# A graph attention kernel: the edge features' products as two halves of 64 rows, in steps of four tiles

## The chip, the cores and the metric

The kernel runs on one core of a Trainium2 chip. A core has five engines, each with its own queue of instructions that it works off in order: TensorE (PE in the profile; its weight loads are listed apart as PEld), VectorE (DVE), ScalarE (ACT), GpSimd (POOL) and SyncE (SP), which here only issues DMAs. Semaphores hold an instruction back until another engine or a DMA has finished. Matmuls read SBUF and write PSUM, a memory of eight banks, each 2 KB on each of 128 partitions (512 f32 values). The metric is the time of one execution on the device in microseconds.

## The reference

One layer of a graph network. There are 12500 nodes with 128 features and 412500 edges, sorted by their target `dst`. Cut to what matters:

```python
h = relu(layernorm(x))
q, k, v = h @ Wq + bq, h @ Wk + bk, h @ Wv + bv        # per node
eh = edge_attr_64 @ We + be                            # per edge, 64 features
attn_in = concat([q[src], k[dst], eh], axis=-1)
hmid = leaky_relu(attn_in @ A1 + b1, 0.2)
scores = leaky_relu(hmid @ A2 + b2, 0.2)               # 8 heads
w = softmax(scores.mean(axis=-1), axis=0)              # over all edges
out = segment_sum(w[:, None] * v[dst], src)            # per source node
y = h @ Wn + bn + out
return x + gamma * (y - mean(y)) / sqrt(var(y) + 1e-5) + beta
```

The product with `A1` is linear, so the kernel folds it into the weights: `Wq`, `Wk` and `We` are multiplied by their part of `A1` once, and an edge's hidden row is the sum of a row for the source, a row for the target and the edge features times a 64x128 matrix.

## The kernel before

Edges are cut into tiles of 128, and eight tiles make a group (`SUPER`); there are 403 groups. Four chunks of 86, 121, 121 and 75 groups (`CHUNKS`) are worked on one after the other.

After a prologue (weights, indices, L243 to L338) and the per-node products (`nodes`, L529), the main part runs in five stages, c = 0 to 4 (the loop at L982). Each stage interleaves several jobs, written as Python generators:

- `first_stage(c)` (L631) makes, for each edge of chunk c, a row of 257 numbers: the place of the source within its block, 128 hidden values (target's part plus edge features' part) and 128 values `v[dst]`. The row is scattered into a table in HBM (`tab`), sorted by source.
- `second_stage` (L692) reads the table of chunk c-1 back block by block, adds the source's part, applies the leaky ReLUs, the heads and a running softmax, and sums the weighted values per source node.
- `ready` (L513) works out ahead, for chunk c+1 (in stage 0 also for what is left of chunk 0), in which slot of the table every edge goes: `count`, `plan`, `place_slots`. Its matmuls are at L459, DVE's reduction of them at L503 and the next selection at L452.
- `clear_ends` clears the ends of the next table.

`interleave` (L61) gives each job a number of steps and always runs the one that is proportionally furthest behind, up to its next `yield`. The order that comes out is the order of the instructions on PE, DVE, ACT and SP (`manual_schedule`, L996). `first_stage` has four yields for a group of eight tiles, in the kernel before and after the change.

A group's data are loaded two groups ahead (`load`, L640): `ea_t`, the edge features, transposed on the host, with tiles 0 to 3 of the group in partitions 0 to 63 and tiles 4 to 7 in partitions 64 to 127; `kv`, a window of target rows, each f32 number split into three bf16 parts; and `offs`, from which DVE makes the 0/1 matrix `sel` (L657).

One step of `first_stage` (L674 to L689) handles two tiles, k and k+4 of the group. The weight matrix `w_ea` has the shape [128, 2, 128] and is block diagonal: the folded 64x128 matrix stands in rows 0 to 63 for the first 128 columns and in rows 64 to 127 for the second, with zeros elsewhere (L241, L257). So one matmul of 128 rows with 256 columns (L679) gives the edge part of both tiles, in one PSUM bank (`row_ps`, two buffers, L610). Two bf16 matmuls with `sel` (L682) add the targets' part and the values. An f32 matmul is carried out as two weight loads and two passes, so L679 has two records for each matmul. `Later` (L80) holds the eviction back by one step: at the start of the next step `evict` (L660) issues on ACT a copy of the places (L662) and a copy of the whole bank (L665) into a row buffer (`pr`, seven buffers), and POOL issues two scatters (L621).

Of the other work, these lines matter here. Second stage, on PE: `turn` L738 and L741, the heads L758, `by_slot` L775, `turn_top` L792, `spread_top` L799, `products` L833. On ACT: `steep` L749, the exponentials L810. On DVE: L750.

## Time and profile before

| | |
|---|---|
| median of 11 runs | 6851.04 us (6835.54 to 6861.52) |
| profiled execution, its own time | 6852.19 us |
| its span in the profile | 6850.4 us |
| mean granted TensorE clock | 0.88 of full speed |
| stage 0: first stage of chunk 0, `ready` | 470 to 1510 us |
| stage 1: first stage of chunk 1, second of chunk 0, `ready` | 1515 to 3110 us |
| stage 2: first stage of chunk 2, second of chunk 1, `ready` | 3115 to 4780 us |
| stage 3: first stage of chunk 3, second of chunk 2 | 4785 to 5930 us |
| stage 4: second stage of chunk 3, then the ending | 5930 to 6850 us |

The stages' limits are read from the first and last L679 of each chunk. How to read the lines: a line of groups gives the source line, engine, operation, tiles (out<-in), form and number of instructions, then the busy time in us, the mean duration in ns, and the engine's idle time just before these instructions with what ended most of it. A line of the windows gives start and end, length, then the busy us and number of instructions of PE, PEld, DVE, ACT and POOL, the granted clock, the share of the DMA engines and GB/s. A line of the timeline gives start and duration in us, engine, line, operation and number; in brackets stands the idle time before it. A line of the waits gives who waited for whom: us in total, times, and the longest. The recorded duration of a matmul includes the tail of its pipeline, so matmuls that follow each other overlap in the records; what a matmul costs in a stream is the distance from start to start.

### The profile page before, as it was taken

What the parts mean: (1) busy time and instruction counts of PE and PEld (TensorE: products, weight loads), DVE (VectorE), ACT (ScalarE), POOL (GpSimd) and SP (SyncE); (2) the same over time, 40 slices, a digit from 0 to 9 for tenths busy, and PEclk for the clock granted to TensorE, in tenths of its full rate; (3) what the DMA queues carried; (4) which work ended last, traced back from release to release, by engine and by line L of the source; (5) the groups of instructions that cost most, each with busy time, mean ns of one, the idle gap of its engine ahead of it and who ended that gap; (6) DMA issues with size and microseconds to landing.
All of it is one profiled execution on the core that took longest, in us unless ns stands there. A gap on an engine that the chain in (4) does not pass through costs nothing. (4 is left out here: it accounts for less than half of the span.)

```text
span 6850.4 us, 98826 instructions
## 1 busy us (share of the span) xinstructions
PE 5186.3 (76%) x31430; PEld 3515.3 (51%) x31788; DVE 4548.1 (66%) x14001; ACT 2187.3 (32%) x5624; POOL 3370.3 (49%) x3236
## 2 busy tenths in 40 slices
PE   0555566558877878788888888777999999888881
PEld 0223343325555555556555555555666666656651
DVE  4875565546666666666666666665777777777778
ACT  0442222223333333333333333333333333333331
POOL 0017667765666666665566665655555555300000
PEclk9777767767889988898999998998999999999995
DMA  9344445556777777676777777776777887644443
GB/s 184 124 164 152 151 136 159 154 154 198 213 213 217 217 214 212 212 218 208 225 235 240 236 241 218 225 223 202 241 252 248 250 257 246 200 153 153 150 145 113
DMA packets 607898, 1362.10 MB, mean 199 GB/s; under 512 B 120437, under 2 KB 337197, under 8 KB 569353
## 3 DMA queue, kind: packets, MB, share of 16 engines
q1 hardware_dynamic: 423284, 877.57, 45.5%
q0 software_dynamic: 154704, 424.26, 17.3%
q10 hardware_dynamic: 29380, 53.87, 2.3%
q8 instruction: 252, 4.13, 0.3%
q14 instruction: 278, 2.27, 0.1%
HBM read 782.14 MB, written 573.14 MB: 198 GB/s over the span
## 5 line engine op out<-in xcount | busy, mean ns | idle before, releaser
L621 POOL DMA_INDIRECT tab<-row,slots x3223 | 3368.6, 1045 | 2545.0 <-issue 827.0
L665 ACT ACTIVATE row<-row_ps 128x512 f32<-128x512 f32 x1612 | 952.0, 591 | 1514.5 <-PE row_ps L682 625.5
L679 PE MATMUL row_ps<-w_ea,ea_t 128*128 128x256 f32 x3224 | 1117.0, 432 | 97.6 <-ACT row L665 55.2
L833 PE MATMUL o_ps<-rows_of,w 128*128 128x128 f32 x7252 | 1121.9, 298 | 76.4 <-DVE w L824 55.1
L750 DVE TENSOR_TENSOR rows_of<-h_ps,low 128x512 f32<-128x512 f32 (+1 forms) x980 | 635.4, 648 | 658.5 <-ACT low L749 406.5
L824 DVE TENSOR_SCALAR w<-iota_f,rows_of,score 128x128 f32<-128x128 f32 x3626 | 1021.6, 351 | 9.5
L833 PEld LDWEIGHTS o_ps<-rows_of,w 128*128 128x128 f32 x7252 | 945.5, 200 | 120.1 <-DVE w L824 76.7
L749 ACT ACTIVATE low<-h_ps 128x512 f32<-128x512 f32 (+1 forms) x980 | 551.1, 562 | 1118.0 <-PE h_ps L741 548.1
L679 PEld LDWEIGHTS row_ps<-w_ea,ea_t 128*128 128x128 f32 x3224 | 628.9, 215 | 465.2 <-issue 206.3
L741 PE MATMUL h_ps<-sel_q,qw 128*128 128x512 bf16 (+1 forms) x2582 | 738.7, 373 | 24.0 <-issue 3.4
L503 DVE TENSOR_REDUCE num<-run 128x5 f32<-128x500 f32 x646 | 433.8, 672 | 416.1 <-remote 227.2
L682 PE MATMUL row_ps<-kv,sel 126*128 126x256 bf16 x3224 | 682.7, 296 | 17.4 <-DMA ea_t<-in_ea 15.7
L758 PE MATMUL s_ps<-rows_of,a_sb 128*32 128x512 f32 (+1 forms) x1960 | 522.9, 625 | 139.2 <-DVE most_of L805 69.2
L738 PE MATMUL h_ps<-ident,rows_of 128*128 128x128 f32 x3626 | 591.5, 284 | 0.9 <-issue 0.9
L459 PE MATMUL run<-one,rest_b 128*128 128x500 f16 x642 | 278.3, 433 | 354.2 <-DVE num L503 246.5
L738 PEld LDWEIGHTS h_ps<-ident,rows_of 128*128 128x128 f32 x3626 | 451.8, 147 | 110.9 <-issue 86.4
L682 PEld LDWEIGHTS <-sel 126*128 126x128 bf16 x3224 | 346.3, 107 | 313.4 <-issue 93.4
L775 PEld LDWEIGHTS s_ps<-heads,z 96*128 96x128 f32 (+1 forms) x3136 | 392.4, 194 | 217.3 <-DVE z L769 151.8
L775 PE MATMUL s_ps<-heads,z 96*128 96x3 f32 (+1 forms) x3136 | 411.1, 252 | 109.4 <-DVE z L769 86.0
L765 ACT ACTIVATE z<-s_ps,b_col 64x512 f32<-64x512 f32 (+1 forms) x392 | 267.5, 682 | 639.5 <-PE s_ps L758 376.3
L452 DVE TENSOR_TENSOR one<-bins_b,block 128x500 f16<-128x500 bf16 x646 | 431.3, 668 | 1.7 <-PE run L459 1.6
L769 DVE SCALAR_TENSOR_TENSOR z<-z 64x512 f32<-64x512 f32 (+1 forms) x392 | 267.4, 682 | 223.1 <-ACT z L765 192.0
(172 smaller groups left out, 4860.2 us busy)
## 6 DMA issues: line engine op xcount, KB each, us to landing
rows_of<-tab SPq DMA_DIRECT2D x196, 1413.5 KB
ea_t<-in_ea SPq DMA_DIRECT2D x403, 256.0 KB
tab<-blank SPq DMA_DIRECT2D x392, 257.0 KB
rows_of<-tab SPq DMA_DIRECT2D x98, 1028.0 KB
rows_of<-tab SPq DMA_DIRECT2D x98, 899.5 KB
tab<-row,slots POOLq DMA_INDIRECT x3223
offs<-off_d SPq DMA_DIRECT2D x403, 126.0 KB
qw<-q_tab SPq DMA_DIRECT2D x392, 96.0 KB
```

The lines of the kernel that those rows point to most:

```text
L621: i = nc.gpsimd.indirect_dma_start(out=tabs[c][:, :], out_offset=bass.IndirectOffsetOnAxis(ap=slots[c][t // (8 * STR)][:m, t % (8 * STR):t ...
L665: nc.scalar.activation(row[:, :, 1:ROW], bank, AF.Copy)
L679: nc.tensor.matmul(bank[:, :, 0:D], lhsT=ea_g[:, ts(k, P)], rhs=w_ea, start=True, stop=False, skip_group_check=True)
L682: nc.tensor.matmul(bank[:, b, :], lhsT=sel[:, ts(b * halves + k, P)], rhs=kv, start=False, stop=True, skip_group_check=True)
L738: nc.tensor.matmul(h_ps[:, ts(j, P)], lhsT=rows_of[i][:, q * QUAD + j, 1:D + 1], rhs=ident, is_transpose=True, start=j == 0, stop=False, s ...
L741: nc.tensor.matmul(h_ps[:, 0:m * P], lhsT=qws[i][:, ts(k, D)], rhs=plss[i][:, q * QUAD * P:(q * QUAD + m) * P], start=False, stop=k == 2, ...
L749: nc.scalar.activation(low, h_ps, AF.Copy, scale=SLOPE)
L750: nc.vector.tensor_max(rows_of[i][:, q * QUAD:q * QUAD + m, 1:D + 1], h_ps.rearrange("p (j e) -> p j e", j=m), low.rearrange("p (j e) -> p ...
L758: nc.tensor.matmul(state["s_ps"][32 * q:32 * (q + 1), 0:m * P], lhsT=a2_sb, rhs=rows_of[i][:, q * QUAD:q * QUAD + m, 1:D + 1], start=True, ...
L775: nc.tensor.matmul(state["s_ps"][:, 0:nq * QUAD].rearrange("p (q j) -> p j q", j=QUAD)[:, j, :], lhsT=state["z"][:32 * nq, ts(j, P)], rhs= ...
L824: nc.vector.tensor_scalar(w, iota_f, rows_of[i][:, t, 0:1], state["score", i][:, t:t + 1], op0=ALU.is_equal, op1=ALU.mult)
L833: nc.tensor.matmul(state["o_ps"][:, 0:D], lhsT=w, rhs=rows_of[i][:, t, D + 1:ROW], start=t == 0, stop=t == ct - 1)
```

## The change

`w_ea` becomes [128, 128]: the folded 64x128 matrix stands in rows 0 to 63 and again in rows 64 to 127, without zeros. A step handles four tiles, k, k+1 and k+4, k+5, with k = 0 or 2. Each tile has its own f32 matmul of 64 rows and 128 columns: tiles k and k+1 use the lower 64 rows of the array and write the first bank, tiles k+4 and k+5 use the upper 64 rows and write the second. They are issued alternately, lower, upper, lower, upper; the four bf16 matmuls follow. A step has two yields: after the first one the two banks are evicted, each with two ACT copies and two scatters. The number of buffers, loads, bf16 matmuls, evictions and scatters is as before, `row_ps` still has two buffers, and the loads and the selection stay at the same yield of a group. In `other_edges` only the slice of `w_ea` is written differently.

```diff
-    w_ea = const.tile([P, 2, D], FP, name="w_ea")
+    w_ea = const.tile([P, D], FP, name="w_ea")
...
-    nc.vector.memset(w_ea, 0.0)
...
-        for b in range(2):
-            nc.vector.tensor_copy(w_ea[b * DE:(b + 1) * DE, b, :], fold[b * DE:(b + 1) * DE, 2, :])
+        nc.vector.tensor_copy(w_ea, fold[:, 2, :])
...
         def evict(g, k, bank):
             row = pr.tile([P, 2, ROW], FP, name="row")
-            nc.scalar.activation(row[:, :, 0:1],
-                                 place1[:, g * SUPER:(g + 1) * SUPER].rearrange("p (b k) -> p b k", b=2)[:, :, k:k + 1],
-                                 AF.Copy)
+            nc.scalar.activation(row[:, :, 0:1], place1[:, g * SUPER + k:g * SUPER + k + 2].unsqueeze(2), AF.Copy)
             nc.scalar.activation(row[:, :, 1:ROW], bank, AF.Copy)
-            for b in range(2):
-                scatter(c, g, b * halves + k, row[:, b, :], sent)
+            for j in range(2):
+                scatter(c, g, k + j, row[:, j, :], sent)
...
-            for k in range(halves):
-                later.step()
+            for k in range(0, halves, 2):
 
                 ea_g, kv, sel = got[g]
-                bank = ps_row.tile([P, 2, 2 * D], FP, name="row_ps")
-                nc.tensor.matmul(bank[:, :, 0:D], lhsT=ea_g[:, ts(k, P)], rhs=w_ea, start=True, stop=False,
-                                 skip_group_check=True)
+                banks = [ps_row.tile([P, 2, 2 * D], FP, name="row_ps") for _ in range(2)]
+                for j in range(2):
+                    for b in range(2):
+                        nc.tensor.matmul(banks[b][:, j, 0:D], lhsT=ea_g[b * DE:(b + 1) * DE, ts(k + j, P)],
+                                         rhs=w_ea[b * DE:(b + 1) * DE, :], start=j == 0, stop=False,
+                                         skip_group_check=True)
                 for b in range(2):
-                    nc.tensor.matmul(bank[:, b, :], lhsT=sel[:, ts(b * halves + k, P)], rhs=kv, start=False, stop=True,
-                                     skip_group_check=True)
-                later.after(1, lambda g=g, k=k, bank=bank: evict(g, k, bank))
+                    for j in range(2):
+                        nc.tensor.matmul(banks[b][:, j, :], lhsT=sel[:, ts(b * halves + k + j, P)], rhs=kv, start=False,
+                                         stop=True, skip_group_check=True)
                 if k == 0 and g + 2 < g0 + n:
                     load(g + 2)
-                if k == 1 and g + 1 < g0 + n:
+                yield
+                for b in range(2):
+                    evict(g, b * halves + k, banks[b])
+                if k == 0 and g + 1 < g0 + n:
                     select(g + 1)
                 yield
-        yield from later.rest()
```

More of the change, by code (lines that the diff above doesn't have):

```diff
@@ L77, in some_steps @@
         yield
-class Later:
-    def __init__(self):
-        self.now = 0
-        self.todo = {}
-    def after(self, steps, job):
-        self.todo.setdefault(self.now + steps, []).append(job)
-    def step(self):
-        self.now += 1
-        for job in self.todo.pop(self.now, []):
-            job()
-    def rest(self):
-        while self.todo:
-            self.step()
-            yield
 @with_exitstack
@@ L635, in first_stage @@
         win_v = kv_tab.rearrange("n (s d) -> (n s) d", s=3)
-        later = Later()
         got = {}
@@ L942, in other_edges @@
                     nc.tensor.matmul(bank[:, 0:D], lhsT=ea_t[b * DE:(b + 1) * DE, ts(j, P)],
-                                     rhs=w_ea[b * DE:(b + 1) * DE, b, :], start=True, stop=True)
+                                     rhs=w_ea[b * DE:(b + 1) * DE, :], start=True, stop=True)
                     nc.vector.tensor_add(hid, hid, bank[:, 0:D])
```

## The prediction

> **What bounds the kernel now.** I read the page first, then the busy time by stretch (one stretch for each of the five stages of the main part), the waits, and last the order of time around the products that change. The chain that ended last covers only the closing normalisation, so it does not help here.
>
> ```profile
> PE 5186.3 (76%) x31430; PEld 3515.3 (51%) x31788; DVE 4548.1 (66%) x14001; ACT 2187.3 (32%) x5624; POOL 3370.3 (49%) x3236
> PEclk9777767767889988898999998998999999999995
> L621 POOL DMA_INDIRECT tab<-row,slots x3223 | 3368.6, 1045 | 2545.0 <-issue 827.0
> L665 ACT ACTIVATE row<-row_ps 128x512 f32<-128x512 f32 x1612 | 952.0, 591 | 1514.5 <-PE row_ps L682 625.5
> L679 PE MATMUL row_ps<-w_ea,ea_t 128*128 128x256 f32 x3224 | 1117.0, 432 | 97.6 <-ACT row L665 55.2
> L682 PE MATMUL row_ps<-kv,sel 126*128 126x256 bf16 x3224 | 682.7, 296 | 17.4 <-DMA ea_t<-in_ea 15.7
> ```
>
> TensorE (PE) has the most work, and L679, which the change rewrites, is among its largest groups. L679 has 3224 records for 1612 matmuls: an f32 matmul is two weight loads and two passes. The stages, with PE, weight loads, DVE, ACT and POOL busy, then the granted clock:
>
> ```profile
> 470.00:1510.00 1040.00, 614.40 (x2961) 338.85 (x2962) 599.82 (x1641) 240.34 (x690) 705.86 (x678) 0.71 0.50 152
> 1515.00:3110.00 1595.00, 1275.12 (x7532) 868.61 (x7634) 1008.70 (x3253) 528.56 (x1448) 1014.29 (x975) 0.87 0.72 211
> 3115.00:4780.00 1665.00, 1366.95 (x8511) 968.34 (x8617) 1055.65 (x3321) 574.37 (x1551) 1015.05 (x968) 0.92 0.74 227
> 4785.00:5930.00 1145.00, 1059.56 (x7024) 777.81 (x7124) 821.90 (x2644) 445.88 (x1193) 626.51 (x597) 1.00 0.77 246
> 5930.00:6850.00 920.00, 680.46 (x4328) 466.91 (x4377) 726.32 (x2362) 255.18 (x544) 3.00 (x3) 0.91 0.46 144
> ```
>
> Stage 0 (to 1510) belongs to POOL: 706 us of scatters and 0.30 us of issue before each of 678 make 909 of 1040 us. In stages 1 to 3 PE is busiest, 80, 82 and 93% of the time. Stage 4 has none of the changed work. Now the order of time: pieces from stages 1 and 3.
>
> ```profile
> 2511.83 0.37 PE L459 MATMUL run<-one,first_b 128*128 128x500 f16 x1
> 2512.13 0.29 PEld L799 LDWEIGHTS s_ps<-top_of,ones 1*128 1x128 f32 x2 [0.41 <-issue]
> 2512.44 0.97 PEld L833 LDWEIGHTS o_ps<-rows_of,w 128*128 128x128 f32 x8
> ...
> 2516.41 0.59 PE L679 MATMUL row_ps<-w_ea,ea_t 128*128 128x256 f32 x2
> 2516.84 0.38 PE L682 MATMUL row_ps<-kv,sel 126*128 126x256 bf16 x2
> 2517.06 0.60 PE L738 MATMUL h_ps<-ident,rows_of 128*128 128x128 f32 x4
> ...
> 5201.43 1.25 PE L758 MATMUL s_ps<-rows_of,a_sb 128*32 128x512 f32 x6
> ...
> 5204.48 0.95 PE L775 MATMUL s_ps<-heads,z 96*128 96x3 f32 x8
> 5205.26 0.97 PEld L833 LDWEIGHTS o_ps<-rows_of,w 128*128 128x128 f32 x8
> ```
>
> Three things are to be seen. First, a step of two tiles costs PE 0.65 us: 2516.41 to 2516.84 for the two 256-column f32 passes (0.215 each), then 0.22 for two bf16 matmuls; their weight loads are hidden. Second, tiles of the array can run side by side: at 5201.43 six passes of L758 (32 columns of the array each, four of 512 and two of 384 columns) take 1.25 us, where one after the other they would take 4 x 0.43 + 2 x 0.32 = 2.36. Third, switching between tile sizes is not free. L799 uses one row. Its weight load comes 0.30 us after the start of L459, whose 500 columns stream in 0.21; so 0.09 passes with nothing streamed, and a load of 0.11 stands open before the first pass. A load that needs no switch starts beside the pass ahead of it: after L775 with 96 rows, L833's load begins 0.17 us before L775's modelled end (5205.43).
>
> **The change part by part.** All counts are per new step of four tiles; there are 806, of which 172 in stage 0, 242 each in stages 1 and 2, and 150 in stage 3.
>
> *Products of the edge features.* Removed: two matmuls, four passes of 256 columns at 0.215 = 0.86 us. Added: four matmuls of 64 rows and 128 columns, eight passes. A pass of 128 columns with its own f32 load spaces at 0.11 (2512.44: eight loads of L833, 0.97 us with the tail of the last). No row shows lower and upper rows at once. One end: side by side, four rounds x 0.11 = 0.44, saving 0.42. Other end: one after the other, 8 x 0.11 = 0.89, costing 0.03. I take side by side, as L758 is the nearest row: its loads also overlap. The bf16 products are the same in number and size.
>
> *Switches.* Two per step: into 64 rows, and back for L682. In: 0.09 + 0.11 = 0.20 by the L799 row. Out: the 64-row L775 at 2507.03 in stage 1 is followed by L833's load only 0.07 us before L775's modelled end, 0.10 later than after 96 rows; with a bf16 load of 0.03 to 0.10 I take 0.15. Together 0.35, with 0 as the lower end where PE waits there anyway and 0.45 as the upper.
>
> The Trainium skill, "TensorEngine Tiling (Array Packing)", Key Properties, says that changing the tiling mode drains the engine, which speaks against this change; it gives no price, and the L799 and L775 rows agree and price it. The skill's "TensorE: Matmul & The Clock Gate", Part 3, has packed tiles finish within one matmul plus about 4 ns for each further tile, and shows no price for a switch; by that alone the step would save 0.42 and stages 1 to 3 some 290 us of PE work. By the rows above nearly all of it is spent again.
>
> *Net on PE*: -0.42 + 0.35 = -0.07 us at full clock. Divided by the granted clocks: 242 x 0.07 / 0.87 + 242 x 0.07 / 0.92 + 150 x 0.07 = 48 us less PE work in stages 1 to 3. PE's gaps end on DVE and ACT, so not all of that reaches the end; busy shares of 80 to 93% count the tails of pipelined passes, and I pass on 0.65: **-31 us** (0 to -45).
>
> *The two PSUM banks.* Before, step k fills one bank while the other is evicted; the bank is needed again two steps later. Now both banks are filled in one step and both evictions (2 x (0.20 + 0.60) = 1.6 us of ACT) must end before the next step, at the place in the queues where before one eviction stood. The waits say how often that binds now:
>
> ```profile
> ACT row L665 <- PE row_ps L682: 625.5, 350, 9.5
> PEld row_ps L679 <- ACT row L665: 117.5, 93, 4.1
> PE row_ps L679 <- ACT row L665: 55.2, 30, 3.8
> ```
>
> I took from the trace, for every even step, the start of L679 two steps later less the start of the eviction less 1.6 us. Median slack is 1.2, 2.1, 2.1 and 3.2 us in stages 0 to 3; the shortfalls add up to 6, 13, 12 and 0 us: **+30 us** (0, if PE then waits less elsewhere; 170, as much again as the 173 us in the last two lines, if ACT comes later than now). Behind a waiting L679 stand PE's whole next products, so the wait is not hidden; behind the waiting eviction stand L749 and L810 on ACT.
>
> *Bunching.* The first eviction of a pair waits for a step that ends about 0.6 us later; the second comes a yield earlier than now. Work that hid a wait in every yield now lies in every second one. If it covers a wait in both, nothing changes; the ends are -0.1 and +0.2 us a step over 634 steps (a sixth and a third of the 0.6 us moved), -60 and +130. I take **+20**. The scatters stay at 3223 and come four at a time; 4 x 1.27 us fits in a step of 6 to 7.7 us, and seven row buffers hold 14 tiles, so POOL's order costs nothing; without that reserve POOL would stand for the 1.2 us of a step's products. SP's loads and DVE's selection keep their yield, so they cost nothing; the sums do not count the prologue (one 128x256 clear and one of two small copies go), under 1 us.
>
> *Stage 0.* There a yield has two L459 matmuls and then L679, beside DVE's L503 (0.68) and L452 (0.67). The products of four tiles at 0.20 + 0.44 + 0.15 + 0.44 = 1.23 us stick out of that cover by about 0.3 where 0.65 did not: 172 x 0.3 = 52 us, half of it under POOL's 87%: **+26** (0 to 75).
>
> Sum: -31 + 30 + 20 + 26 = +45 on the profiled execution's 6852.2, which is 1.2 above the median of 6851.0: **6895 us**.
>
> **The rivals.**
>
> *Serial halves (slower, about 7170).* If lower and upper rows run one after the other, loads or passes, a step costs +0.03 + 0.35 = 0.38 more. Stages 1 to 3: 0.38 x 691 (634 steps divided by their clocks) x 0.65 = 171; stage 0: products of 1.68 us stick out by 0.75, 172 x 0.75 x 0.5 = 65; both evictions start 0.45 later still, so banks 60; bunching 20: +316. For it: no row shows two row halves at once, and L833's loads already space the passes at 0.11, so loads that queue would do it alone. Against it: L758. Between 7050 and 7300.
>
> *The switches are hidden (faster, about 6750).* The place is the start of the step: 437 of L679's loads (344 ended by "issue", 93 by ACT) already follow an idle weight loader, and a drain there is free. If half of the switch time falls into such gaps, PE saves 0.42 - 0.17 = 0.25 a step: 0.25 x 691 x 0.65 = 112, and with little bunching (-20) and stage 0 hidden under POOL, less 30 for the banks: about -100. It decides from 0.17 us of switch cost a step downward. Against: three steps in four have no gap there. Between 6680 and 6837.
>
> *It does not do what it says*: side by side, but the time stays in ACT's and DVE's round trips, so nothing shows: 6851, part of the first case's own range.
>
> **How the numbers follow.** A measurement of this kernel can tell about 0.2%, 14 us. Chances: the forecast case (6840 to 6980) 0.52, serial halves 0.23, hidden switches 0.25. Range: 6775 to 7190 leaves out about a tenth at each end. Faster: 0.24 of the hidden switches and 0.03 of the forecast case, 0.27. Same: 0.14 of the forecast case and 0.01, 0.15. Slower: the rest, 0.58.
>
> **What would show it.** In the profile after: the edge products with 64 rows, twice the records, busy time about half of 1117 us if side by side and near it or above if serial; their first load some 0.09 us after the streams ahead of it; L682's first load about as late behind them; PE waiting for ACT's row longer than 173 us in total, by less than 60; stage 0 longer by 20 to 60 us, stages 1 to 3 within 30 us each. I am wrong if stages 1 to 3 shrink by over 100 us (switches cheaper), or grow by over 150 (serial, or the banks bind).

## The result, and the profile after

The changed kernel takes 7030.5 us (median of 9 runs, 7010.0 to 7060.4), the kernel before 6851.6 us beside it (median of 34). The ratio is 1.0268, with a 95% interval of 1.0254 to 1.0282: 2.7% slower, 179 us. The profiled execution took 7065.6 us, its span is 7063.7 us, its mean granted clock 0.842 of full speed.

The page of the kernel after, the lines that answer to those shown of before (L597 is now the scatter, L639 the eviction, L654 the edge products, L659 the products with `sel`):

```profile
PE 5269.2 (75%) x34652; PEld 3444.9 (49%) x35012; DVE 4544.7 (64%) x13999; ACT 2163.3 (31%) x5624; POOL 3341.9 (47%) x3236
PEclk9776666566888888888899988888999999999995
L597 POOL DMA_INDIRECT tab<-row,slots x3223 | 3340.1, 1036 | 2786.5 <-ACT row L638 1023.9
L639 ACT ACTIVATE row<-row_ps 128x512 f32<-128x512 f32 x1612 | 945.6, 591 | 1545.2 <-PE row_ps L659 568.1
L654 PE MATMUL row_ps<-w_ea,ea_t 64*128 64x128 f32 x6448 | 729.7, 346 | 71.4 <-ACT row L639 29.4
L659 PE MATMUL row_ps<-kv,sel 126*128 126x256 bf16 x3224 | 586.4, 313 | 19.4 <-DMA offs<-off_d 15.2
```

The edge products have twice the records and busy time falls from 1117.0 to 729.7 us; yet the program is longer, and the POOL line has a new main reason to be idle, the place copy L638. No engine has become busier in a way that would explain 179 us: DVE, ACT and POOL are each busy for a little less than before. The time is in waits. The windows of the five stages (columns as in the table before):

```profile
472.00:1556.00 1084.00, 634.43 (x3657) 319.52 (x3657) 604.49 (x1654) 226.63 (x691) 711.09 (x682) 0.62 0.48 147
1562.00:3209.00 1647.00, 1297.59 (x8470) 840.13 (x8576) 1004.01 (x3231) 522.46 (x1442) 997.25 (x967) 0.81 0.69 203
3225.00:4922.00 1697.00, 1370.81 (x9431) 952.51 (x9537) 1045.16 (x3296) 564.20 (x1543) 993.09 (x961) 0.88 0.71 222
4942.00:6137.00 1195.00, 1079.77 (x7585) 760.37 (x7684) 815.78 (x2628) 444.93 (x1185) 616.52 (x595) 0.98 0.74 235
6138.00:7063.00 925.00, 686.32 (x4357) 471.06 (x4408) 730.74 (x2375) 257.65 (x551) 4.63 (x4) 0.91 0.45 143
```

Measured from the first eviction of one chunk to that of the next, the stages last 1076, 1664, 1722, 1192 and 922 us, against 1035, 1598, 1676, 1138 and 920 before: +41, +66, +46, +54 and +2. Every stage that has a changed step loses, and the one without loses nothing.

One new step in stage 3, from the timeline of PE and its weight loads:

```profile
5202.69 0.81 PE L719 MATMUL h_ps<-sel_q,qw 128*128 128x512 bf16 x2
5203.43 0.52 PEld L654 LDWEIGHTS row_ps<-w_ea,ea_t 64*128 64x128 f32 x8 [0.42 <-issue]
5203.43 0.72 PE L654 MATMUL row_ps<-w_ea,ea_t 64*128 64x128 f32 x8
5204.08 0.33 PEld L659 LDWEIGHTS <-sel 126*128 126x128 bf16 x4
5204.08 0.61 PE L659 MATMUL row_ps<-kv,sel 126*128 126x256 bf16 x4
5204.53 0.95 PE L753 MATMUL s_ps<-heads,z 96*128 96x3 f32 x8
```

In the single records the eight passes of L654 start at 5203.433 and .440, .647 and .653, .758 and .765, .870 and .877: always a lower and an upper one 7 ns apart, and the pairs 0.11 us apart (the first pair's 0.21 holds its own load). So the halves do run side by side. The last pass of L719 starts at 5203.124; at 0.21 us for its 512 columns (L459 streams 500 in that time) its stream ends at about 5203.34, and the first load of L654 begins some 0.09 us later. The load of L659 begins at 5204.077, 0.20 us after the start of the last pass. Over all 806 steps the medians are the same: 7 ns within a pair, 0.20 us from the last pass to that load. From the end of L719's stream to the start of the next work at 5204.53 the step costs PE 1.19 us, where before four tiles cost two steps of 0.65. On PE the change does what it says, and saves a little.

The waits of the kernel after (who waited for whom, us in total, times, longest):

```profile
POOL tab L597 <- ACT row L638: 1023.9, 399, 12.8
ACT low L727 <- PE h_ps L719: 654.4, 460, 18.8
ACT row L639 <- PE row_ps L659: 568.1, 242, 14.3
DVE rows_of L728 <- ACT low L727: 523.4, 433, 6.8
ACT row L639 <- remote: 459.7, 97, 13.5
POOL tab L597 <- ACT row L639: 449.5, 143, 18.2
PEld row_ps L654 <- ACT row L639: 61.2, 74, 5.3
PE row_ps L654 <- ACT row L639: 29.4, 29, 4.8
```

The lines of the kernel before that answer to these, besides those that the prediction shows:

```profile
POOL tab L621 <- ACT row L665: 771.2, 357, 17.7
ACT low L749 <- PE h_ps L741: 548.1, 467, 16.2
POOL tab L621 <- ACT row L662: 427.0, 204, 7.5
DVE rows_of L750 <- ACT low L749: 406.5, 411, 4.6
ACT row L665 <- remote: 314.7, 66, 15.2
```

PE's two waits for the banks, the last two lines of the kernel after, add up to 91 us, against 173 before: they shrank. POOL's waits for ACT's two copies grew from 1198 us together to 1473. The second stage's chain waits longer too: ACT 654 us for the hidden rows of L719 (548 before, on L741), and DVE 523 us for ACT's result (407 before). Those products have nothing to do with the edge features; they stand behind a step of four tiles in PE's queue.

The word "remote" in the fifth line is a wait whose releaser the profile does not find among the instructions that ended just then. The kernel before had it too (ACT's eviction, the last line above). The timeline of before, in stage 0, shows what it is:

```profile
1009.55 0.57 PE L459 MATMUL run<-one,first_b 128*128 128x500 f16 x1
...
1010.77 0.64 PE L682 MATMUL row_ps<-kv,sel 126*128 126x256 bf16 x2
...
1013.22 0.60 ACT L665 ACTIVATE row<-row_ps 128x512 f32<-128x512 f32 x1 [5.70 <-issue]
...
1016.76 0.68 DVE L503 TENSOR_REDUCE num<-run 128x5 f32<-128x500 f32 x1 [6.48 <-remote]
```

DVE's reduction starts 6.6 us after the modelled end of the matmul it reads (1009.55 + 0.57 = 1010.12), and the records name nothing else that it waits for. PE's word that a matmul is done is seen by ACT and DVE microseconds after that modelled end. Whether the word is late or the matmul ends later than modelled, the records do not tell; it is called a late signal here in either case. Matmul records that a profile lacks are not the reason: of the kernels below, `bunch_only` has 358 matmuls fewer than weight loads (31430 and 31788) and no such wait, `after_again` has as many of one as of the other (35012) and does wait. This becomes important below.

### The profile page after: what moved, and what is told of

It reads as the page before. It is cut to its first block, busy times and chain, and to the rows that moved or that the text cites. A ratio compares the mean times of both kernels' runs of the same rounds, so it can differ in the third digit from the quotient of the medians.

```text
span 7063.7 us, 105224 instructions
## 1 busy us (share of the span) xinstructions
PE 5269.2 (75%) x34652; PEld 3444.9 (49%) x35012; DVE 4544.7 (64%) x13999; ACT 2163.3 (31%) x5624; POOL 3341.9 (47%) x3236
## 5 line engine op out<-in xcount | busy, mean ns | idle before, releaser
L597 POOL DMA_INDIRECT tab<-row,slots x3223 | 3340.1, 1036 | 2786.5 <-ACT row L638 1023.9
L639 ACT ACTIVATE row<-row_ps 128x512 f32<-128x512 f32 x1612 | 945.6, 591 | 1545.2 <-PE row_ps L659 568.1
L811 PE MATMUL o_ps<-rows_of,w 128*128 128x128 f32 x7252 | 1143.5, 302 | 67.4 <-DVE w L802 49.2
L719 PE MATMUL h_ps<-sel_q,qw 128*128 128x512 bf16 (+1 forms) x2580 | 774.4, 388 | 26.1 <-issue 7.9
L654 PE MATMUL row_ps<-w_ea,ea_t 64*128 64x128 f32 x6448 | 729.7, 346 | 71.4 <-ACT row L639 29.4
L654 PEld LDWEIGHTS row_ps<-w_ea,ea_t 64*128 64x128 f32 x6448 | 542.4, 227 | 487.2 <-issue 347.2
L736 PE MATMUL s_ps<-rows_of,a_sb 128*32 128x512 f32 (+1 forms) x1960 | 546.5, 638 | 157.7 <-DVE most_of L783 80.4
L716 PE MATMUL h_ps<-ident,rows_of 128*128 128x128 f32 x3626 | 617.6, 293 | 0.2 <-issue 0.2
L435 PE MATMUL run<-one,rest_b 128*128 128x500 f16 x642 | 304.5, 474 | 404.4 <-DVE num L479 340.3
L659 PE MATMUL row_ps<-kv,sel 126*128 126x256 bf16 x3224 | 586.4, 313 | 19.4 <-DMA offs<-off_d 15.2
L719 PEld LDWEIGHTS <-qw 128*128 128x128 bf16 x2940 | 305.9, 104 | 136.3 <-issue 32.0
```

Source lines behind the costliest of these rows:

```text
L597: i = nc.gpsimd.indirect_dma_start(out=tabs[c][:, :], out_offset=bass.IndirectOffsetOnAxis(ap=slots[c][t // (8 * STR)][:m, t % (8 * STR):t ...
L639: nc.scalar.activation(row[:, :, 1:ROW], bank, AF.Copy)
L654: nc.tensor.matmul(banks[b][:, j, 0:D], lhsT=ea_g[b * DE:(b + 1) * DE, ts(k + j, P)], rhs=w_ea[b * DE:(b + 1) * DE, :], start=j == 0, stop ...
L659: nc.tensor.matmul(banks[b][:, j, :], lhsT=sel[:, ts(b * halves + k + j, P)], rhs=kv, start=False, stop=True, skip_group_check=True)
L716: nc.tensor.matmul(h_ps[:, ts(j, P)], lhsT=rows_of[i][:, q * QUAD + j, 1:D + 1], rhs=ident, is_transpose=True, start=j == 0, stop=False, s ...
L719: nc.tensor.matmul(h_ps[:, 0:m * P], lhsT=qws[i][:, ts(k, D)], rhs=plss[i][:, q * QUAD * P:(q * QUAD + m) * P], start=False, stop=k == 2, ...
```

## The experiments

Four accounts of the lost time were to be told apart: the *bunching* (products in lumps of four tiles, evictions in pairs); the *64-row products* (their switches); the *two banks* that are both filled in a step; and PE's *work and clock*. No kernel here leaves work out; those that do something twice overwrite the first result with the same values. Ratios are of neighbouring runs of both kernels and so can differ by 0.2% from the ratio of the medians. The groups below did not all run on the same chip, and two kinds of chip appeared: in three sets of runs the kernel before takes 6133 to 6213 us and the traces show no late signals, in three others (that of the result among them) it takes 6749 to 6865 us and they show them. So each number is compared with the kernel before in its own set of runs. The two later sets with late signals ran on the same chip, and there the kernel before took 6749 us in the one and 6865 in the other; which chip gave the result is not on record.

### One part of the change alone, and more work

The new schedule with the old products (`bunch_only`, its diff against the changed kernel): four tiles a step, two banks, evictions in pairs after the first yield, but 128-row products with the block-diagonal weights.

```diff
+                for j in range(2):
+                    nc.tensor.matmul(banks[j][:, :, 0:D], lhsT=ea_g[:, ts(k + j, P)], rhs=w_ea, start=True, stop=False,
+                                     skip_group_check=True)
...
-                    evict(g, b * halves + k, banks[b])
+                    evict(g, k + j, banks[j])
```

> The changed kernel's schedule (steps of four tiles, both banks filled at once, both evicted half a step later) with the products of before: block-diagonal weights, 128 rows, 256 columns, no switch of the array's tiling. Theory A, the bunching costs the time: it is as slow as the changed kernel, 7030 us, or up to 50 us more, since its products take PE about 0.11 us a step longer than the 64-row ones (1.30 against 1.19). Theory B, the 64-row halves cost it (switches, or a lower granted clock because half the passes are gone): 6850 to 6880 us, clock near 0.88. A mixture lies between.

The new products with the old schedule (`rows64_only`, again against the changed kernel): a step of two tiles, the eviction a step later through `Later`, both tiles of a step in the same row half, so with the switches and without anything side by side.

```diff
+            for k in range(halves):
+                later.step()
...
+                b = k // 2
                 for j in range(2):
+                    nc.tensor.matmul(bank[:, j, 0:D], lhsT=ea_g[b * DE:(b + 1) * DE, ts(k % 2 * 2 + j, P)],
+                                     rhs=w_ea[b * DE:(b + 1) * DE, :], start=j == 0, stop=False, skip_group_check=True)
...
+                later.after(1, lambda g=g, k=k, bank=bank: evict(g, 2 * k, bank))
```

> The schedule of before (two tiles a step, one bank, evicted one step later) with products of 64 rows: both tiles of a step come from the same half, so their passes run one after the other into one bank, as long as before (0.44 us), and only the two switches of the array's tiling are added, 0.32 us for each of 1612 steps. If a switch costs what the profile after shows and two thirds of PE's time reach the end: 0.32 x 1382 (the 1268 steps of stages 1 to 3 over their clocks) x 0.65 = 290 us more, 7140 us. Theory A takes this price. Theory B with dear switches: over 7250 us. If drains fall into waits that are there anyway: under 6950 us.

The edge products of the changed kernel issued twice (`after_twice`, first diff), and those of the kernel before issued twice (`before_twice`, second diff).

```diff
-                for j in range(2):
+                for j in (0, 1, 0, 1):
                     for b in range(2):
                         nc.tensor.matmul(banks[b][:, j, 0:D], ...)
```

```diff
-                nc.tensor.matmul(bank[:, :, 0:D], lhsT=ea_g[:, ts(k, P)], rhs=w_ea, ...)
+                for _ in range(2):
+                    nc.tensor.matmul(bank[:, :, 0:D], lhsT=ea_g[:, ts(k, P)], rhs=w_ea, ...)
```

> The changed kernel with its edge products issued twice (the second pair overwrites the first): PE gets 0.44 us more in each step, no further switch, no other wait. It measures how much of PE's time in a step reaches the end. At 0.65 and 691 steps (of stages 1 to 3, over their clocks): 200 us more, 7230 us. Theory B as a clock effect (PE too idle, so its clock is granted less): the added activity raises the clock from 0.84 towards 0.88 and the time stays within 50 us of 7030 or falls. Theory A: 7130 to 7250 us.

> The kernel before with its edge product issued twice in every step (the second overwrites the first): PE gets 0.43 us more in each of 1612 steps. It measures how much of PE's time reaches the end in the schedule of before. At 0.65 and 1382 steps: 386 us more, 7240 us. If PE's time is mostly hidden behind the waits for DVE and ACT, under 7000 us, and then the changed kernel's saving of 0.11 us a step could not show either; if PE is the bound, 7400 us.

Measured on a chip without late signals (before: 6207.1 us):

| kernel | median us | ratio, 95% interval | clock |
|---|---|---|---|
| `bunch_only` | 6263.8 | 1.0074 (1.0050 to 1.0099) | 0.907 |
| `rows64_only` | 6270.3 | 1.0080 (1.0049 to 1.0110) | 0.888 |
| `after_twice` | 6293.7 | 1.0127 (1.0106 to 1.0149) | 0.925 |
| `before_twice` | 6294.7 | 1.0129 (1.0107 to 1.0151) | 0.948 |

What follows: the schedule alone costs 0.74%, with no 64-row product in it. And PE's work is cheap on this chip. `before_twice` adds 0.43 us to each of the 1268 old steps of stages 1 to 3; divided by a clock of about 0.92 (that of `before_half` below) that is 593 us, and the program grows by 88 us: 0.15 of it. `rows64_only` adds 0.32 us a step (the two switches, by the timeline above the 0.42 that passes side by side save less the 0.11 that a step saves in all, so 0.31, and four passes at 0.11 for two at 0.215), 441 us, and the program grows by 63: 0.14. Doubling PE's edge products costs 1.3%, doing them in lumps 0.7%. Nor does the clock set the price: the two doubled kernels have the highest clocks and the longest times. It does move the shares: with the added work of `before_twice` it rose (0.911 to 0.917 in the runs of before), which gives some of the time back, and in `rows64_only` it fell to 0.888. And the shares hold for a chip on which another engine, POOL, is full for half of the program; this is shown below.

### The banks, and the evictions in pairs

The changed kernel again, beside three variants of when it evicts. `evict_now` evicts both banks before the first yield, so that they come free earlier:

```diff
+                for b in range(2):
+                    evict(g, b * halves + k, banks[b])
                 if k == 0 and g + 2 < g0 + n:
                     load(g + 2)
                 yield
-                for b in range(2):
-                    evict(g, b * halves + k, banks[b])
```

`quarter_split` has four yields in a step (and twice as many steps told to `interleave`), and one eviction after the first, the other after the third. `quarter_both` is its control: four yields too, both evictions after the second, where the changed kernel has them.

```diff
                 yield
-                for b in range(2):
-                    evict(g, b * halves + k, banks[b])
+                evict(g, k, banks[0])
+                yield
                 if k == 0 and g + 1 < g0 + n:
                     select(g + 1)
                 yield
+                evict(g, halves + k, banks[1])
+                yield
```

> The changed kernel itself, beside the kernel before on the chip of these runs. The chip of the first result had waits for PE that no record explains (before: 532 us on ACT, 471 us on DVE; after: 720 and 539); the chip of the first four experiments had none, and the kernel before took 6207 us there. If the change's price is the bunching alone (theory A), the ratio on such a chip is that of the bunched schedule with the products of before, 1.007, or up to 0.005 less. If the 64-row halves cost something of their own (theory B: fewer passes, a lower granted clock), it is above 1.012. If the chip plays no part, 1.027.

> The changed kernel with both evictions issued in the yield of the products, not half a step later: ACT waits for the products at the head of its queue, and the banks come free earlier. If what costs is PE waiting for the banks, it is faster than the changed kernel by up to 30 us. If what costs is ACT held up in front of the second stage's work (L749 and what follows it), it is slower than the changed kernel by 50 us or more. If the lumping of PE's products costs, within 20 us of it.

> The changed kernel with four yields a step: products at the first, the first bank evicted a quarter step later, the second three quarters later, so that evictions and scatters come two and two, evenly, as before the change, and only PE's products stay lumped. If the evictions in pairs (ACT, POOL) are the price of the bunching, most of it is gone: at most 0.3% over the kernel before on the same chip. If PE's lump is the price, it stays within 20 us of the changed kernel, or is slower because the second bank is late.

> The control for the split evictions: four yields a step, but products at the first and both evictions at the third, which is half a step later as in the changed kernel. It should be within 15 us of the changed kernel; what it is off by is the price of the finer interleaving itself and is to be taken from the split one.

Measured on a chip with late signals (before: 6749.4 us):

| kernel | median us | ratio, 95% interval |
|---|---|---|
| `after_again` | 6931.4 | 1.0283 (1.0238 to 1.0328) |
| `evict_now` | 7041.1 | 1.0434 (1.0394 to 1.0473) |
| `quarter_split` | 6855.8 | 1.0167 (1.0131 to 1.0203) |
| `quarter_both` | 6923.8 | 1.0258 (1.0206 to 1.0310) |

Freeing the banks earlier makes it 110 us worse. The wait of ACT's eviction for the products, in `after_again` and then in `evict_now`:

```profile
ACT row L639 <- PE row_ps L659: 560.0, 230, 11.8
```

```profile
ACT row L639 <- PE row_ps L659: 1544.6, 474, 15.0
```

ACT now stands at the eviction for 1545 us instead of 560, with the second stage's work behind it in its queue. This kernel changes two things at once, but the earlier banks at least are no gain: what a step delays in ACT's queue weighs more. Spreading the evictions takes 68 us off against its control (6923.8 to 6855.8), of the 182 us between `after_again` and before; finer yields alone give 8 us, which is within the intervals.

### The same on a chip without late signals

The changed kernel, the bunched old products, these with the evictions spread as in `quarter_split` (`bunch_split`), and the kernel before with its eviction in a half step of its own instead of through `Later` (`before_half`, the diff below is against the kernel before). `after_c` and `bunch_c` are the changed kernel and `bunch_only` again; `bunch_split` is `bunch_only` with the yields of `quarter_split`.

```diff
-                later.step()
...
-                later.after(1, lambda g=g, k=k, bank=bank: evict(g, k, bank))
...
+                yield
+                evict(g, k, bank)
...
                 yield
-        yield from later.rest()
```

> The changed kernel beside the bunched schedule with the products of before, for the first time on the same chip. Theory A (the bunching is the price, whatever the products): the two are within 0.5% of each other, 1.020 to 1.030 on a chip with late PE signals, about 1.007 on one without. Theory B (the 64-row halves have a price of their own): the changed kernel is over 1% above the other.

> The same kernel as bunch_only (the changed schedule, the products of before), to be set against the changed kernel on this chip. Theory A: within 0.5% of the changed kernel. Theory B: 1.005 to 1.010 over the kernel before on any chip, and the changed kernel over 1% above it.

> As bunch_c, with four yields a step: both products at the first yield, the first bank evicted a quarter step later, the second three quarters later. With the changed products, splitting the evictions took 1% off. Theory A (pairs of evictions on ACT): at most 0.5% over the kernel before, the rest being PE's lump. If PE's lump is most of the price, within 0.3% of bunch_c.

> The kernel before with two yields for each step of two tiles: products, half a step, eviction, half a step. Nothing is lumped; the eviction comes half a step later instead of a whole one. If the delay to the eviction matters by itself (ACT held up in front of the second stage's work), it is slower than before by 0.5 to 1.5%. If lumps alone matter, it is within 0.5% of the kernel before, or faster, since the banks come free earlier.

Measured (before: 6133.2 us):

| kernel | median us | ratio, 95% interval | clock | stages 0 to 3, us |
|---|---|---|---|---|
| `before_half` | 6130.6 | 0.9996 (0.9983 to 1.0009) | 0.921 | 935, 1318, 1400, 1090 |
| `after_c` | 6180.1 | 1.0085 (1.0068 to 1.0101) | 0.881 | 929, 1325, 1404, 1116 |
| `bunch_c` | 6194.6 | 1.0096 (1.0078 to 1.0113) | 0.909 | 933, 1331, 1407, 1134 |
| `bunch_split` | 6175.6 | 1.0071 (1.0054 to 1.0088) | 0.915 | 928, 1319, 1403, 1134 |

Here the changed kernel loses 0.85%, 47 us. `bunch_c` repeats `bunch_only`: +61 us from the schedule. With the 64-row products in it, `after_c` is 14 us faster than `bunch_c`, at a lower clock; the intervals overlap, but the sign is that of the work saved on PE. Evicting half a step later is no cost in itself: `before_half` is level with before, so its trace can stand for before on this chip. Most of the loss is in stage 3, +44 us for `bunch_c` and +26 for `after_c`. The waits of `before_half`, then of `bunch_c`, then of `after_c`:

```profile
ACT low L748 <- PE h_ps L740: 503.0, 675, 2.9
PEld row_ps L678 <- ACT row L665: 368.2, 220, 5.1
PE row_ps L678 <- ACT row L665: 223.4, 128, 4.6
```

```profile
ACT low L728 <- PE h_ps L720: 875.6, 666, 18.5
PEld row_ps L656 <- ACT row L642: 255.1, 225, 4.6
PE row_ps L656 <- ACT row L642: 147.5, 115, 4.2
```

```profile
ACT low L727 <- PE h_ps L719: 884.6, 669, 19.0
PEld row_ps L654 <- ACT row L639: 193.2, 211, 5.7
PE row_ps L654 <- ACT row L639: 96.3, 95, 5.5
```

PE's wait for the banks falls from 592 us to 403 and 290: on this chip too the banks do not bind more (`before_half` evicts later than the kernel before, so this comparison is with `before_half` alone). The wait that takes its place is that of ACT's leaky ReLU (`low`) for the hidden rows: about as often, 503 to some 880 us, its longest from 2.9 to 19 us. Not all of it counts (ACT's wait for its eviction falls at the same time from 876 us to 545 in `after_c`), but it has the mark of a lump: the same number of waits, longer ones.

Why most of the loss is in stage 3 can be read from the windows. The first two are stages 1 and 3 of `before_half`, the third is stage 3 of `bunch_c`:

```profile
1411.00:2729.00 1318.00, 1164.29 (x7621) 811.20 (x7620) 1001.99 (x3247) 533.55 (x1446) 1004.61 (x973) 0.95 0.85 255
4130.00:5219.00 1089.00, 1051.80 (x7131) 776.69 (x7131) 818.39 (x2648) 469.14 (x1192) 639.12 (x599) 0.99 0.80 260
4142.00:5277.00 1135.00, 1076.74 (x7090) 793.32 (x7088) 816.79 (x2632) 446.27 (x1190) 621.47 (x597) 0.98 0.76 247
```

Between two of POOL's scatters lie 0.30 us even where nothing is waited for (the "issue" that the prediction counts in stage 0), and the busy time does not count them. With 0.30 us for each of 973 scatters POOL is taken up for 1005 + 292 = 1297 of the 1318 us of stage 1, or 98%. The same sum gives 98% in stage 0, 94% in stage 2 and 75% in stage 3. So on a chip without late signals POOL bounds stages 0 and 1 and nearly stage 2, and PE and ACT can lose time there that does not show; only in stage 3 has POOL room.

### The same on a chip with late signals

The kernel before, the changed kernel, `bunch_only` and `rows64_only` again, under the names `before_d`, `after_d`, `bunch_d` and `rows64_d`.

> The kernel before, for its profile on this chip: whether PE's signals come late here, and the stages' lengths beside which the other three are set. On a chip without late signals about 6130 to 6210 us, on one with them 6740 to 6860 us.

> The changed kernel on this chip: 1.007 to 1.010 over the kernel before on a chip without late PE signals, 1.024 to 1.032 on one with them.

> The changed schedule with the products of before. On a chip with late PE signals: if the bunching is what is made dearer there, it is within 0.5% of the changed kernel (1.022 to 1.033); if the 64-row halves are (their tenth more PE instructions, or the lower clock), it is at 1.005 to 1.015. On a chip without: about 1.009.

> The schedule of before with 64-row products one after the other: as many PE instructions as the changed kernel, twice its switches, no bunching. On a chip with late PE signals: if the 64-row halves or the number of instructions is what is made dearer there, 1.020 or more; if the bunching is, 1.005 to 1.015. On a chip without: about 1.008.

Measured (before: 6864.5 us; `before_d`, one run, 6846.0). "Late" is the total of ACT's and DVE's "remote" waits in the profiled execution:

| kernel | median us | ratio, 95% interval | clock | late us, ACT and DVE | stages 0 to 3, us |
|---|---|---|---|---|---|
| `before_d` | 6846.0 | | 0.885 | 540, 434 | 1034, 1590, 1669, 1147 |
| `after_d` | 7041.8 | 1.0261 (1.0235 to 1.0287) | 0.847 | 618, 467 | 1078, 1648, 1693, 1191 |
| `bunch_d` | 7065.1 | 1.0304 (1.0273 to 1.0336) | 0.873 | 646, 537 | 1065, 1674, 1713, 1190 |
| `rows64_d` | 6971.9 | 1.0142 (1.0109 to 1.0176) | 0.855 | 293, 316 | 1057, 1634, 1711, 1173 |

The bunched kernels lose three to four times as much as without late signals: the schedule alone 201 us, and with the 64-row products 23 us less, again at a lower clock (the intervals overlap). `rows64_d` loses 107 us, against 63 there. Stage 1 shows what the schedule does; its window in `before_d` and in `bunch_d`:

```profile
1524.00:3115.00 1591.00, 1269.56 (x7541) 860.79 (x7642) 1010.27 (x3256) 527.69 (x1448) 1007.92 (x971) 0.88 0.73 213
```

```profile
1553.00:3227.00 1674.00, 1297.18 (x7535) 888.56 (x7635) 1010.94 (x3246) 523.04 (x1447) 999.19 (x975) 0.85 0.70 202
```

83 us longer with the same instructions and the same busy time on DVE, ACT and POOL; PE's 28 us more go with its clock. What is added is idle time on every engine, and here POOL has room for it: by the sum above it is taken up for 1299 of the 1591 us of stage 1 (82%), and for 89, 78 and 70% in stages 0, 2 and 3. Set side by side by stage, the schedule alone costs -2, 13, 7 and 44 us without late signals (`bunch_c` against `before_half`) and 31, 84, 44 and 43 us with them (`bunch_d` against `before_d`). In stage 3, where POOL is not full on either chip and hardly any signal is late (7 waits in `before_d`, 5 in `bunch_d`), the price is the same; in the others it shows where POOL is not the bound. How much of it are late signals can't be read from their totals: they rise by 105 and 103 us in `bunch_d` (two engines' waits, which overlap), by 78 and 33 in `after_d`, and `rows64_d` has six tenths of the late time of before and is still 1.4% slower.

### Undoing the bunching step by step

On a chip without late signals again (before: 6213.2 us), the changed kernel with 64-row products, first with the evictions spread (`quarter_split_e`, the kernel of `quarter_split`), then with the products with `sel` spread too (`spread_split`): those of the first bank in the first quarter of the step, those of the second bank in the second.

```diff
-                for b in range(2):
-                    for j in range(2):
-                        nc.tensor.matmul(banks[b][:, j, :], ...)
+                for j in range(2):
+                    nc.tensor.matmul(banks[0][:, j, :], ...)
...
                 yield
+                for j in range(2):
+                    nc.tensor.matmul(banks[1][:, j, :], ...)
+                evict(g, k, banks[0])
+                yield
```

> The changed kernel with its evictions apart (a quarter and three quarters of a step after the products), as quarter_split, as the control on this chip: 1.013 to 1.020 over the kernel before on a chip with late PE signals, about 1.006 on one without.

> As quarter_split_e, and PE's lump divided too: edge products of the four tiles and the bf16 products of the first bank at the first yield, the bf16 products of the second bank a quarter step later. No instruction is added or taken away. If what is left of the price is PE's lump, it falls by 0.3% or more against quarter_split_e; if the evictions were the whole of it, within 0.2%. Should it come out below the kernel before, it would beat both.

`quarter_split_e` takes 6236.0 us, ratio 1.0046 (1.0031 to 1.0060); `spread_split` 6216.8 us, ratio 1.0007 (0.9996 to 1.0019). With both spread, the loss is gone and the 64-row products remain. The wait of `low`, in `quarter_split_e` and then in `spread_split`:

```profile
ACT low L729 <- PE h_ps L721: 674.4, 639, 8.9
```

```profile
ACT low L731 <- PE h_ps L723: 613.4, 631, 11.5
```

From some 880 us in `after_c` it falls to 674 and 613, back towards the 503 of `before_half` (both of another such chip; the changed kernel itself was not run on this one). No kernel beat before: what PE saves by the side-by-side products is worth too little to show.

## Why the prediction was right or wrong

The sign was right and the range held the result (forecast 6895 with 6775 to 7190, measured 7030), the size was not: 45 us were forecast, 179 came. (The forecast's own terms add up to 6896.)

*Products and switches*: right. Side by side was taken, and the pairs are 7 ns apart. The Trainium skill, "TensorE: Matmul & The Clock Gate", Part 3, gives about 4 ns for each further tile; the trace has 7, and that is nothing beside the 0.11 of a pass. Into the 64 rows was put at 0.20 and measured as 0.09 up to the first load and about 0.1 for that load; out at 0.15, and the load of L659 begins 0.20 after the last pass started, of which 0.11 is the pass. The step takes 1.19 us where 1.23 were forecast, so it saves 0.11 us against two steps of 0.65, not 0.07. The rival of serial halves falls by the 7 ns. It would have come near the measured time (7170 was its forecast, and 7050 its lower end), and only the timeline tells that it is not what happened.

*"I pass on 0.65"*: too high, for added and for saved work. Added PE work reaches the end with 0.14 to 0.15 on a chip without late signals (`before_twice`, `rows64_only`), and with 0.23 on one with them (`rows64_d`: 107 us of 0.32 x 1268 / 0.885 = 458). Saved work does about as little: 0.11 us times 634 steps at a clock near 0.9 is 77 us, and `after_c` is 14 us below `bunch_c`: 0.18. On the chip with late signals it is 23 of 81 (0.28). The prediction read PE's 80 to 93% busy as a bound, and for the whole program it is not one. It counted the 0.30 us before a scatter in stage 0 alone; in stage 1 of its own profile POOL with them is taken up for 1014 + 293 = 1307 of 1595 us, 82%, as much as PE, and without late signals for 98%. The low shares on the chips without late signals may be owed to this in part. In stage 3 alone, where POOL has room, more gets through: `before_twice` has 1140 us there against 1090 of `before_half`, 0.4 of the added work, and `after_twice` 1162 against 1116 of `after_c`, 0.7 (single profiles of two such chips; `bunch_only` and `bunch_c` differ by 2 us in that stage). What holds the stages on a chip with late signals was not found out; round trips among PE, ACT and DVE fit the waits, but that is argued. By the shares of the whole program the rival of hidden switches was wrong by more than its premise: even 0.25 us saved a step would have brought some 30 to 50 us and not 112.

*The two banks, +30*: not found. PE's waits for ACT's row fell, from 173 to 91 us here and from 592 to 290 where signals are not late, and freeing the banks earlier made the kernel slower. The shortfalls that the prediction counted assumed that everything else keeps its time.

*"Bunching ... I take +20" (-60 to +130)*: this is the step that failed. It assumed that work which hid a wait in every yield covers one as well in every second. All that belongs to the schedule was forecast at 20 + 30 + 26 = 76 us. On a chip such as the predicted one it measured +201 us (`bunch_d`), of which 171 in stages 1 to 3 against the 20 of this term, beyond its upper end of 130. Where PE's signals are not late, the schedule alone measured +61 us (`bunch_c`), and with the halves +47 where +45 had been forecast. That this is near is luck: the forecast was made from the other kind of chip, put 26 us into stage 0 and 19 into stages 1 to 3, and 44 of the 61 came in stage 3. That the schedule is the cause is shown by these kernels; how it works inside a stage is argued from the waits: ACT's leaky ReLU waits behind a lump of four tiles on PE and behind two evictions in its own queue, and DVE waits for ACT. Undoing the lumps undid the loss without late signals, 19 us and again 19 us (`bunch_split` against `bunch_c`, `spread_split` against `quarter_split_e`); with them, spreading the evictions alone took off 68 us of 182.

*Stage 0, +26*: about right in size on the predicted chip (+41 there, +44 and +31 in `after_d` and `bunch_d`), inside its 0 to 75; without late signals it is -6. *Stages 1 to 3 within 30 us each*: wrong, +66, +46 and +54. For a growth over 150 the prediction named two causes, serial halves or binding banks, and it was neither.

What was missed in the profile of before: the "remote" waits. ACT and DVE there wait some 520 and 460 us in all for signals that come after PE's modelled end, nearly all in stages 0 to 2. A round trip with such a signal is longer than the durations of its instructions, so an order with less cover for it can lose more than the durations say. That the changed kernel loses 2.6 to 2.8% where these signals appear and 0.85% where they do not is measured, and so is that POOL is nearly full in stages 0 to 2 where they do not; that the late signals are what takes the stages off POOL's bound is only argued. The late time moves otherwise than the program does (`rows64_d`), stage 3 has next to no late signals and yet lost 54 us here against 26 on the other kind of chip, and the chips may differ in other things. What makes the signals late, and which part of the remaining 1.7% of `quarter_split` on such a chip is PE's lump and which the 64 rows, stays open; `spread_split` was not run there.

## What to carry to other kernels

A busy share of 80 or 90% does not make an engine the bound: add up each engine's busy time and its fixed gaps by stage (POOL's 0.30 us before every scatter here), and double one operation and see what the program takes, before counting on a saving. What such a test gives holds for the chip and the stage that it was made on. Doing the same work in steps twice as large costs by itself, here 0.7 to 3%; a gain that needs the larger step has to pay for that first, or the step has to be spread again over the yields. Compare variants on the same chip and side by side: the same kernel before took 6133 us on one chip and 6865 on another, and 6749 and 6865 in two sets on one; the loss was 0.85% where it took 6133 and 2.6% where it took 6865.

## What the runs showed of the hardware that was not expected

- Two halves of 64 rows overlap wholly, f32 weight loads included: eight passes with eight loads start within 0.44 us, in pairs 7 ns apart. The Trainium skill, "TensorEngine Tiling (Array Packing)", Key Properties, says that different tiles can load and multiply in parallel and that a change of mode drains the engine; both are seen, and the time with nothing streamed or loaded is 0.09 us on the way into 64 rows.
- In three of six sets of runs, two of them on one chip, PE's signals to ACT and DVE come late, nearly always in stages 0 to 2: waits of up to 15 us, about 980 us in all in the kernel before. In the other three, on three chips, the traces show none, and the kernel before takes 8 to 11% less.
- Doubling the edge products of the kernel before added some 593 us of work to PE (the estimate above) and 88 us to the program, and the granted clock rose from 0.911 to 0.917 to 0.948.
- A scatter on POOL took 1.03 us (1004.6 us for 973 in stage 1 of `before_half`) and, where it waited for nothing, the next one started 0.30 us after it, so scatters with these gaps fill 98% of that stage although POOL's busy share is 76%.
